# A long-lived pool on the other side of SBUF, residual pieces at later marks, and another opening order for attention, in a four-layer graph network kernel

## The chip, the core and the metric

The kernel is one launch on one core of one Trainium2 chip. The metric is the device time in microseconds (us), the median of the runs shown. A core has five engines that run their own instruction streams: TensorE (PE in the profile, with PEld for its weight loads), VectorE (DVE), ScalarE (ACT), GpSimd (POOL) and SyncE (SP). In this kernel SP does hardly anything but issue DMAs. On every engine the program's order is the order of execution, so an instruction that waits holds up all behind it on its engine.

## The reference, cut to what matters

x is 128 batches of 64 nodes with 256 channels in float32. Each of four layers adds its result to x. All of them begin with a norm over channels and a ReLU.

```python
h = relu(layernorm(x)); x = x + L0(h, adj)   # aggregate, W1, batch norm, ReLU, W2, batch norm
h = relu(layernorm(x)); x = x + L1(h, adj)   # two graph convolutions, then LSTMs
h = relu(layernorm(x)); x = x + L2(h)        # one head of causal attention over 64 nodes
h = relu(layernorm(x)); x = x + L3(h, adj)   # four heads of attention, masked by adj
# inside L1: for p = 1, 2, 3, 4 an LSTM over windows of p nodes replaces the last node of each window
```

## The kernel before, in words

The 8,192 rows are 16 chunks of 512 (`NCH`); two neighbours make a super-chunk (`SUP` = 2), so layer 1 has eight stages, sc = 0 to 7. The products of weight matrices are computed in Strassen's way with seven products, which is why so many small sums and copies on DVE, ACT and POOL stand between the matmuls.

**Pools.** SBUF has two stacks, left and right, and `pool(name, bufs, side)` opens a pool on top of one. A tile that comes to lie where older tiles lay waits for the last users of those. Layer 0 has `z1b` (64 KB per partition: 4 KB for each chunk), `w0` and, later, `stage` on the left, and `l0b` (24 KB) on the right: `w2_sb` (4 KB), `w2_sums` (4 KB) and two buffers of tag `h1` (8 KB each). Layer 1 then opens `lasting` (18 KB: `wg0_sb`, `wg1_sb` of 2 KB, `wih1_4` of 6 KB, two `cv` buffers of 4 KB), `w1` (46.5 KB: the third part of the single LSTM's weights and six buffers `wset` of 7 KB), `l1` (40 KB, its first tile `early`/`gates` of 16 KB) and, on the right, `l1r`. `lasting` lives until the end of the kernel.

**The opening of layer 1.** SP issues, in this order, `wg0_sb`, `wg1_sb` (in the profile `wg_sb`, L870 and L871), two bias loads (L874, L875), the two loads of x into `early` (L968), the single LSTM's weights (L888 to L890) and six `wset` loads (L905). `first_convolutions` makes chunks 0 and 1: tokens by transposes (L253), the sum with x (L979), a norm, and the aggregation (L228). Filler transposes (`keep_busy`) keep PE occupied in between.

**The stages of layer 1.** The LSTMs of a stage are a generator, `lstms(sc, hT)`. It stops at marks that are numbered through: 0 to 3 in the LSTM with p = 1 (`single`, matmuls at L1369), 4 to 7 in p = 2, 8 to 13 in p = 3, 14 to 21 in p = 4; half marks (4.5, 5.5, 8.5, 9.5, 11.5 ...) lie where a step's last product of its first two gates has been issued. At each mark the other work of the stage is taken one piece at a time from other generators, by tables of marks:

- `convolutions(c)`, 16 pieces: scale (L918); transposes (L1009), put to DRAM (L261), get (L268) and the load of x (L1016); `add_squares` (L298); two pieces of the norm's statistics (L195); two of its application on ACT (L210); aggregation (L228); copies (L1026); a product, its bound, a second product, its bias, an aggregation; and two pieces that write hT (L961). Tables `FIRST` (sc 0), `CONV`, and for the first pieces, taken a stage earlier, `BEGUN` and `BEGUN_FIRST` (sc 0).
- `residual(c)`, 3 pieces: four transposes of hT (L1309) and a put; a get; `add_squares` into x. Table `RESIDUAL`.
- `ahead(c)`, 7 pieces: a put and a get that put x in another order; two of statistics; two of application; transposes and a put. Tables `AHEAD`, `LATE`, `LATEST`, `FINAL`.

When several tables name one mark, the pieces run in this order: convolutions of the next stage, residual, ahead, begun convolutions.

**Weights.** Each p > 1 needs four `wset` tiles (gates in the order 0, 2, 3, 1), loaded by SP (L905) in a ring of six buffers: two in a p's last step just behind its half mark, two at its end. The two that are issued behind mark 11.5 are those of p = 4 for its third and fourth gates. p = 4 begins with a product for gates 0, 2 and 3 in turn (L1134, into y, y and x).

```python
each(A, pe(4), do("act", 2), do("act", 1))
yield "a"                        # a half mark: the pieces of that mark run here
each(B[:1], pe(3))
if last:
    load_sets(2)                 # two wset loads, L905, on SP
```

**The opening of attention.** Steps with names are written in an order by hand (`FIRST` in the last section, then `THIRD`, `ROUND` ...), `name+c` being step `name` for chunk c. `res1` and `pair1` are the pieces of the last two residuals and their reordering; `keep` puts x to DRAM; `norm3`, `apply3`, `chan3` are layer 3's norm, its application and PE transposes (L240); `q3x`, `k3x` its first products (L1528 on `w_sb`); `weights3` loads that weight (L1972); `load3` gets the transposed h of a later chunk. The step `table` is an Exp of one column (L1977).

Of the kernel before, what the change touches and what calls it, by code (L numbers as in the profile page):

```python
# [8 lines left out]
F32 = mybir.dt.float32  # L9
AF = mybir.ActivationFunctionType  # L10
# [3 lines left out]
P = 128  # L14
# [5 lines left out]
def kernel(  # L20
# [22 lines left out]
    nc = tc.nc  # L43
# [13 lines left out]
    SUP = 2  # L57
# [9 lines left out]
    small = ctx.enter_context(tc.tile_pool(name="small", bufs=4))  # L67

    def pool(name, bufs, side="left"):


        stack = ExitStack()
        return stack.enter_context(tc.tile_pool(name=name, bufs=bufs, side=side,
                                                reuse_waits="tile")), stack.close
# [72 lines left out]
    def keep_busy(n, name):  # L147

        ps = bank(f"idle_{name}")
        for i in range(n):  # L150
            nc.tensor.transpose(ps[:, :P], ident, ident)
# [106 lines left out]
    def put(mid, name, tag="far", bufs=12):  # L258

        far = dram.tile([P, Q, CH * KD // Q], F32, tag=tag, name=f"far_{name}", bufs=bufs)  # L260
        nc.sync.dma_start(far, mid)  # L261
        return far

    def get(dst, far):

        src = far.rearrange("(a t) b n -> b t a n", a=Q)
        for b in range(Q):
            nc.sync.dma_start(dst[b * 32 : (b + 1) * 32], src[b])  # L268
# [21 lines left out]
    def add_squares(dst, base, src):  # L290

        for h in range(2):
            q = slice(h * Q // 2, (h + 1) * Q // 2)

            def part(a):
                return a.rearrange("p j (k q c) -> p q (j k) c", k=KD, q=Q)[:, q]

            nc.vector.tensor_add(part(dst), part(base), src[:, q].rearrange("p q (n c) -> p q n c", c=32))  # L298
# [304 lines left out]
    with tc.manual_schedule(engines={mybir.EngineType.PE, mybir.EngineType.DVE,  # L603
# [69 lines left out]
        c = NCH - 1  # L673
# [175 lines left out]
    with tc.manual_schedule(engines={mybir.EngineType.PE}):  # L849
        c = NCH - 1  # L850
# [10 lines left out]


    xs = {}
    lasting, close_lasting = pool("lasting", 1)
    w1, close_w1 = pool("w1", 1)
    l1, close_l1 = pool("l1", 2)
    l1r, close_l1r = pool("l1r", 2, "right")
# [42 lines left out]
    hTs = {}  # L910
# [392 lines left out]
    def residual(c, hT):  # L1303

        i = c % SUP
        mid = l1r.tile([P, Q, CH * KD // Q], F32, tag="g", name=f"hm_{c}", bufs=3)
        for k in range(KD):
            for e in range(2):
                nc.vector.transpose(  # L1309
                    mid.rearrange("p (e h) (j k c) -> p k e j h c", e=2, j=NJ, k=KD)[:, k, e],  # L1310
                    hT[:, k, :].rearrange("p (h t i j e) -> p i e j h t", h=Q // 2, i=SUP, j=NJ,
                                          e=2)[:, i, e])
        far = put(mid, f"h{c}")
        yield
        dst = hT[:, i, :].rearrange("p (q n) -> p q n", q=Q)
        get(dst, far)
        yield
        add_squares(xs[c], xs[c], dst)
        yield
# [143 lines left out]
    def new_hT(sc):  # L1463

        hTs[sc] = l1r.tile([P, KD, SUP * CH], F32, tag="hT", name=f"hT_{sc}")
# [66 lines left out]
    def begin_attention():  # L1532

        tiles = [shared(f"{n}2_0") for n in ("hT", "q")]
        for w, i in ((wg0_sb, 0), (wg1_sb, 1)):
            nc.sync.dma_start(w, products_far[:, :, i * D : (i + 1) * D])
        load2(0, tiles[0].rearrange("p (q n) -> p q n", q=Q))
        st[0, "q2"] = tiles[1].rearrange("p (k n) -> p k n", k=KD)
        st[0, "v2"] = wih1[0].rearrange("p g s f -> p (g s f)")[:, : NJ * D].rearrange("p (j d) -> p j d", d=D)
        yield  # L1540
        for m in range(KD):
            nc.scalar.copy(st[0, "q2"][:, m, :], project_t(m, st[0, "hT2"], wg0_sb, "q2_0"))
            yield
        for t in range(NJ // 2):
            project_v(st[0, "v2"], st[0, "hT2"], wg1_sb, 0, "2_0", [t])
            yield
        new_hT(last + 1)
        load2(1, hTs[last + 1][:, 1, :].rearrange("p (q n) -> p q n", q=Q))
        st[1, "q2"] = hTs[last + 1][:, 0, :].rearrange("p (k n) -> p k n", k=KD)
        yield  # L1550
        for m in range(KD):
            nc.scalar.copy(st[1, "q2"][:, m, :], project_t(m, st[1, "hT2"], wg0_sb, "q2_1"))
            yield

    EARLY = 0, 3, 5, 7, 9, 9, 13, 15
    RESIDUAL = (0, 4, 5.5), (3, 5, 9)
    CONV = (3, 4, 5, 5.5, 7, 8, 9, 10, 10), (5, 5, 6, 9.5, 11, 11.5, 13, 14, 15, 15.5, 17, 18, 20)
    BEGUN = (11, 11, 14.5, 17, 17, 20, 21), (17.5, 19, 21)
    BEGUN_FIRST = (12, 14.5, 17, 19, 19, 20, 21), (20, 21, 21)
    FIRST = (1, 3, 3, 4, 4.5, 5, 5.5, 7, 8, 9, 9.5, 11, 11.5, 11.5), (2, 5, 8.5, 9, 9.5, 10, 11, 13, 14, 15, 15.5, 17, 17.5, 19, 20, 20)  # L1560
    AHEAD = (6, 7), (9, 10)
    LATE = (4.5, 4.5, 5.5, 9, 19.5), (9.5, 9.5, 11, 12, 21)
    LATEST = (4.5, 4.5, 5.5, 9, 9.5), (9.5, 9.5, 10, 11, 11.5)
    IDLE = {11: 8}
# [4 lines left out]
    with tc.manual_schedule(engines={mybir.EngineType.PE, mybir.EngineType.DVE, mybir.EngineType.Pool,  # L1569
# [3 lines left out]
        convs = {c: (convolutions if c >= SUP else first_convolutions)(c) for c in range(NCH)}  # L1573
# [17 lines left out]
    with tc.manual_schedule(engines={mybir.EngineType.PE, mybir.EngineType.DVE, mybir.EngineType.Pool,  # L1591
                                     mybir.EngineType.Activation, mybir.EngineType.SP}):
        last = NCH // SUP - 1
        lstm_tiles += [l1.tile(shape, F32, tag=tag, name=f"l_{tag}", bufs=1) for tag, shape in (
            ("gates", [P, 4, KD, CH]), ("cell", [P, KD, CH]), ("hs", [P, KD, CH]), ("hd", [P, 4, CH // 2]))]
        for sc in range(last + 1):
            todo = {}

            def units(places, unit):
                for n in places:  # L1600
                    todo.setdefault(n, []).append(unit)


            if sc < last:
                for i in range(SUP):
                    units((CONV if sc else FIRST)[i], convs[(sc + 1) * SUP + i])
                new_hT(sc + 1)
            if sc:
                for i in range(SUP):
                    units(RESIDUAL[i], residual((sc - 1) * SUP + i, hTs[sc - 1]))  # L1610
            else:
                units([0], convs[1])
            if sc > 1:
                for i in range(SUP):
                    units((LATEST if sc == last else LATE)[i], aheads[(sc - 2) * SUP + i])
            if sc:
                for i in range(SUP):
                    units((FINAL if sc == last else AHEAD)[i], aheads[(sc - 1) * SUP + i])
            if sc + 1 < last:
                for i in range(SUP):  # L1620
                    units((BEGUN if sc else BEGUN_FIRST)[i], convs[(sc + 2) * SUP + i])
            if sc == last:
                units(EARLY, begin_attention())
            n = -1
            for mark in lstms(sc, hTs[sc]):
                n = n + 0.5 if mark else int(n) + 1
                for u in todo.pop(n, ()):
                    next(u)
                if sc == last and n in IDLE:
                    keep_busy(IDLE[n], f"l{n}")  # L1630
            assert not todo
# [339 lines left out]
    def weights3(c):  # L1971
        nc.sync.dma_start(w3_sb, w3.rearrange("(k p) f -> p k f", p=P))  # L1972

    @step
    def table(c):

        nc.scalar.activation(small.tile([P, 1], F32, tag="table", name="table"),  # L1977
                             hTs[last][:, 0, :1], AF.Exp)


    ends = {NCH - SUP + i: residual(NCH - SUP + i, hTs[NCH // SUP - 1]) for i in range(SUP)}
    orders = {c: to_pairs(c) for c in ends}
    steps["res1"] = lambda c: next(ends[c])
# [52 lines left out]
    def store(c, t):  # L2036
# [3 lines left out]
        for r in range(2):  # L2040
# [16 lines left out]

    FIRST = """table+0 load2+2 score2+0 res1+14 v2a+1 v2b+1 res1+15 exp2+0 score2+1 divide2+0 q2+2 copyq2+2  # L2060
               exp2+1 turn2+0 divide2+1 load2+3 v2a+2 v2b+2 out2+0 keep+0 weights3+0 res1+14 res1+15 turn2+1
               norm3+0 score2+2 out2+1 keep+1 res1+14 res1+15 exp2+2 apply3+0 back+0 divide2+2 chan3+0
               pair1+14 pair1+14 turn2+2 q30+0 k30+0 norm3+1 pair1+15 pair1+15 out2+2 keep+2 q31+0 k31+0
               apply3+1 square3+1 score3+0 norm3+2 v3a+0 load3+1 v3b+0"""
    LAST = """exp3-2 sum3-2 load3+0 divide3-2 qa-1 q5-1 c11-1 v3a-1 qb-1 c12-1 qc-1 turn3-2 qd-1 out3-2
              score3-1 q30+0 store-2 back-1 k30+0 back+0 exp3-1 q31+0 sum3-1 k31+0 divide3-1 score3h+0
              v3b-1 exp3a+0 sum3a+0 turn3-1 exp3b+0 v3a+0 divide3a+0 out3-1 sum3b+0 divide3b+0 store-1
# [3 lines left out]
    def run(order, c):  # L2071
        for name in order.split():
            i = max(name.find("+"), name.find("-"))
            steps[name[:i]](c + int(name[i:]))

    with tc.manual_schedule(engines={mybir.EngineType.PE, mybir.EngineType.DVE,
                                     mybir.EngineType.Activation, mybir.EngineType.Pool,
                                     mybir.EngineType.SP}):
        run(FIRST, 0)
        close_l1r()  # L2080
        pool3, close_l3 = pool("l3", 2, "right")
# [8 lines left out]
        run(ROUND.replace("load2+1", "").replace("qd-2", "qd-2 sums_h-1"), NCH - 1)  # L2090
        run(LAST, NCH - 1)
    close_l2()
    close_lasting()
    close_l3()
    psum.pop()[2]()


# [44 lines left out]
```

## Time and profile before

| | us |
|---|---|
| median of 3 runs | 1902.86 (1902.72 to 1904.42) |
| profiled execution: its own time | 1900.71 |
| its span | 1898.9 |
| PE busy in the span | 1840.9 (97%) |
| DVE, ACT, POOL busy | 1319.9, 1053.2, 611.6 |
| mean granted PE clock | 0.991 |

A line of the timeline reads: start in us from the span's start, duration, engine and line, operation, output<-inputs, shapes, count; in brackets the idle time of that engine just before it, and what ended it. `SPq` is a DMA issue. A line of the waits view reads: engine, output and line that waited <- who ended it: us in total, times, the longest.

### The profile page before, as it was taken

What the parts mean: (1) busy time and instruction counts of PE and PEld (TensorE: products, weight loads), DVE (VectorE), ACT (ScalarE), POOL (GpSimd) and SP (SyncE); (2) the same over time, 40 slices, a digit from 0 to 9 for tenths busy, and PEclk for the clock granted to TensorE, in tenths of its full rate; (3) what the DMA queues carried; (4) which work ended last, traced back from release to release, by engine and by line L of the source; (5) the groups of instructions that cost most, each with busy time, mean ns of one, the idle gap of its engine ahead of it and who ended that gap; (6) DMA issues with size and microseconds to landing.
All of it is one profiled execution on the core that took longest, in us unless ns stands there. A gap on an engine that the chain in (4) does not pass through costs nothing.

```text
span 1898.9 us, 40682 instructions
## 1 busy us (share of the span) xinstructions
PE 1840.9 (97%) x15463; PEld 1513.1 (80%) x15463; DVE 1319.9 (70%) x3408; ACT 1053.2 (55%) x2502; POOL 611.6 (32%) x856
## 2 busy tenths in 40 slices
PE   8999988998999999999999999999999979999998
PEld 6877856985898799699699789789979847777776
DVE  6768845666667777767867866876667657777776
ACT  5766535555456565665655656656565634444453
POOL 5856623222212322422321422332132203332332
PEclk9999999998999999999999999999999989999999
DMA  3223642133433341432533433342244154444433
GB/s 114 79 69 142 213 182 73 59 110 123 133 134 123 106 161 52 148 127 89 178 123 112 165 118 130 145 131 104 84 133 141 38 162 146 134 151 141 143 112 112
DMA packets 113410, 234.48 MB, mean 123 GB/s; under 512 B 11712, under 2 KB 77120, under 8 KB 113216
## 3 DMA queue, kind: packets, MB, share of 16 engines
q1 hardware_dynamic: 112320, 230.02, 35.9%
q8 instruction: 123, 2.02, 0.4%
q0 software_dynamic: 320, 1.05, 0.2%
q10 hardware_dynamic: 576, 0.82, 0.1%
q14 instruction: 71, 0.58, 0.1%
HBM read 164.21 MB, written 67.63 MB: 122 GB/s over the span
## 4 chain that ended last, share of the span: by engine, by line
PE 83%; DVE 6%; ACT 5%; POOL 2%; issue 1%; DMA 1%; SPq 0%; DVEq 0%; ACTq 0%; POOLq 0%
PE x L1187 22%; PE z L1187 11%; PE v L1521 6%; PE y L1187 6%; PE y L1134 4%; PE v L936 3%; PE u L950 3%; PE p_q L1528 3%; PE X L1825 3%; PE X L437 2%; PE x L1134 2%; PE X L513 2%; PE x L1369 2%; PE y L1369 2%; PE Y L1825 1%
## 5 line engine op out<-in xcount | busy, mean ns | idle before, releaser
L1102 ACT ACTIVATE l_gates<-l_gates,bias 128x256 f32<-128x256 f32 (+4 forms) x528 | 238.1, 498 | 213.8 <-DVE l_gates L1196 111.8
L1187 PE MATMUL x<-xd,wset 128*128 128x128 f32 (+2 forms) x1152 | 255.4, 303 | 2.1 <-ACT l_gates L1193 1.7
L1187 PE MATMUL x<-l_hd,wset 128*128 128x128 f32 (+2 forms) x1152 | 254.6, 303 | 0.0
L1253 POOL TENSOR_TENSOR l_gates<-l_gates 128x512 f32<-128x512 f32 (+2 forms) x48 | 75.2, 1567 | 388.5 <-ACT l_gates L1102 388.5
L1187 PEld LDWEIGHTS x<-xd,wset 128*128 128x128 f32 x1152 | 187.7, 191 | 8.3 <-issue 1.4
L1187 PEld LDWEIGHTS x<-l_hd,wset 128*128 128x128 f32 x1152 | 187.8, 191 | 5.0
L1196 DVE TENSOR_TENSOR l_gates<-l_gates,x 128x128 f32<-128x128 f32 (+2 forms) x384 | 121.2, 321 | 99.8 <-PE x L1187 96.8
L1196 DVE TENSOR_TENSOR l_gates<-l_gates,z 128x128 f32<-128x128 f32 (+2 forms) x384 | 102.4, 318 | 124.3 <-PE z L1187 124.2
L1187 PE MATMUL z<-l_hs,wset 128*128 128x128 f32 (+2 forms) x768 | 147.0, 304 | 0.7 <-DVE l_hs L1111 0.7
L1187 PE MATMUL z<-hT,wset 128*128 128x128 f32 (+2 forms) x768 | 146.3, 303 | 0.0
L1193 ACT COPY l_gates<-y 128x128 f32<-128x128 f32 (+2 forms) x192 | 53.1, 290 | 142.5 <-PE y L1187 137.3
L1187 PEld LDWEIGHTS z<-l_hs,wset 128*128 128x128 f32 x768 | 116.8, 191 | 5.6 <-DVE l_hs L1111 2.3
L1187 PEld LDWEIGHTS z<-hT,wset 128*128 128x128 f32 x768 | 117.1, 191 | 3.3
L1102 ACT ACTIVATE l_gates<-x,bias 128x128 f32<-128x128 f32 (+2 forms) x216 | 84.7, 392 | 31.1 <-PE x L1187 28.4
L1187 PE MATMUL x<-hT,wset 128*128 128x128 f32 (+2 forms) x384 | 85.7, 305 | 0.0
L1187 PE MATMUL x<-l_hs,wset 128*128 128x128 f32 (+2 forms) x384 | 84.9, 303 | 0.0
L327 POOL TENSOR_TENSOR xd<-hT 128x128 f32<-128x128 f32 (+2 forms) x72 | 42.2, 587 | 129.1 <-DVE hT L1113 115.7
L1187 PE MATMUL y<-l_hd,wset 128*128 128x128 f32 (+2 forms) x384 | 83.6, 310 | 0.0
L1187 PE MATMUL y<-xd,wset 128*128 128x128 f32 (+2 forms) x384 | 82.6, 307 | 0.0
L1268 ACT ACTIVATE l_gates<-l_cell 128x256 f32<-128x256 f32 (+2 forms) x144 | 55.2, 383 | 42.5 <-DVE l_cell L1267 42.5
L1643 POOL TENSOR_TENSOR s<-s,mx 128x256 f32<-128x256 f32 (+2 forms) x33 | 40.4, 1225 | 118.9 <-DVE mx L1642 118.9
L1369 PE MATMUL x<-xd,wih 128*128 128x512 f32 x144 | 66.6, 609 | 8.9 <-DVE l_gates L1393 8.7
(358 smaller groups left out, 4557.5 us busy)
## 6 DMA issues: line engine op xcount, KB each, us to landing
wset<-wfar SPq DMA_DIRECT2D x96, 896.0 KB, 6.7
hT<-far_h SPq DMA_DIRECT2D x124, 128.0 KB, 3.2
far_h<-hm SPq DMA_DIRECT2D x16, 512.0 KB, 3.0
far_n<-xs SPq DMA_DIRECT2D x16, 512.0 KB, 4.0
xs<-far_n SPq DMA_DIRECT2D x64, 128.0 KB, 3.3
far_x<-xs SPq DMA_DIRECT2D x16, 512.0 KB, 3.0
x<-far_x SPq DMA_DIRECT2D x64, 128.0 KB, 3.3
xt<-in_x_dram SPq DMA_DIRECT2D x15, 512.0 KB, 3.9
```

The source lines that it names most:

```text
L936: nc.tensor.matmul(banks[m], wg0_sb[:, k, m * P : (m + 1) * P], agg[:, k, :], start=(k == 0), stop=(k == KD - 1))
L950: nc.tensor.matmul(banks[j // 2][:, j % 2, :], v[:, k, j * P : (j + 1) * P], wg1_sb[:, k, :], start=(k == 0), stop=(k == KD - 1))
L1102: nc.scalar.activation(gate(q, c, part), src, AF.Tanh if q == 2 else AF.Sigmoid, bias=bs[:, q * KD + c : q * KD + c + 1])
L1134: nc.tensor.matmul(folded(self.psum(kind)), wsets[p, self.q][:, BLOCKS[kind][0], :], ox[0][kind], start=kind in (1, 5), stop=True, skip_gr ...
L1187: nc.tensor.matmul(folded(self.psum(kind)), wsets[p, self.q][:, BLOCKS[kind][i], :], (ox[self.s] if part == "x" else oh)[kind], start=firs ...
L1196: nc.vector.tensor_add(gate(self.q, *dst), gate(self.q, *a), self.psum(kind))
L1253: nc.gpsimd.tensor_mul(gates[:, 0, :, :n], gates[:, 0, :, :n], gates[:, 2, :, :n])
L1268: nc.scalar.activation(gate(2, c, part), cells[:, c, part], AF.Tanh)
L1369: nc.tensor.matmul(folded(ps(g, kind)), single_block(KINDS1[kind])[:, g, :], right[kind], start=kind in (2, 5, 1), stop=True, skip_group_c ...
L1521: nc.tensor.matmul(ps[:, i, :], hT[:, k, j, :], w[:, k, first : first + D], start=(k == 0), stop=(k == KD - 1))
L1528: nc.tensor.matmul(ps.rearrange("p (a n) -> p a n", n=P), w[:, k, m * P : (m + 1) * P], hT[:, k], start=(k == 0), stop=(k == KD - 1))
L1825: nc.tensor.matmul(st[c, tag][:, i * CH // 2 : (i + 1) * CH // 2].rearrange("p (a n) -> p a n", n=P), w, st[c, "o7"][kind], start=first an ...
```

## The change

Four things change. `lasting` is opened on the right, below which `l1r` then lies; `w1` and `l1` start where `lasting` lay. Tables of marks change: the residual pieces move from (0, 4, 5.5), (3, 5, 9) to (0, 6, 9), (5.5, 7, 9.5) in stages 1 to 6 (stage 7 keeps the old ones under a new name); `AHEAD` moves accordingly; the second begun piece of the even chunk moves from mark 11 to 11.5; stage 0 uses `BEGUN` like all others, with its `FIRST` denser. Attention's opening order is rewritten, with `apply3+0`, `back+0` and `chan3+0` ahead of the gets and sums of `res1`, the Exp of chunk 0 earlier, and `weights3` behind `keep+1`. The step `table` goes.

```diff
-    lasting, close_lasting = pool("lasting", 1)
+    lasting, close_lasting = pool("lasting", 1, "right")
...
-    RESIDUAL = (0, 4, 5.5), (3, 5, 9)
+    RESIDUAL = (0, 6, 9), (5.5, 7, 9.5)
...
-    BEGUN = (11, 11, 14.5, 17, 17, 20, 21), (17.5, 19, 21)
-    BEGUN_FIRST = (12, 14.5, 17, 19, 19, 20, 21), (20, 21, 21)
-    FIRST = (1, 3, 3, 4, 4.5, 5, 5.5, 7, 8, 9, 9.5, 11, 11.5, 11.5), (2, 5, 8.5, 9, 9.5, 10, 11, 13, 14, 15, 15.5, 17, 17.5, 19, 20, 20)
-    AHEAD = (6, 7), (9, 10)
+    BEGUN = (11, 11.5, 14.5, 17, 17, 20, 21), (17.5, 19, 21)
+    RESIDUAL_LAST = (0, 4, 5.5), (3, 5, 9)
+    FIRST = (1, 1, 2, 2, 3, 4, 4, 5, 5.5, 7, 8, 9, 10, 10), (2, 3, 4.5, 5, 5, 6, 9.5, 11, 11.5, 13, 14, 15, 15.5, 17, 18, 20)
+    AHEAD = (9, 10), (10, 11)
...
-                    units(RESIDUAL[i], residual((sc - 1) * SUP + i, hTs[sc - 1]))
+                    units((RESIDUAL_LAST if sc == last else RESIDUAL)[i], residual((sc - 1) * SUP + i, hTs[sc - 1]))
...
-                    units((BEGUN if sc else BEGUN_FIRST)[i], convs[(sc + 2) * SUP + i])
+                    units(BEGUN[i], convs[(sc + 2) * SUP + i])
...
-    @step
-    def table(c):
-
-        nc.scalar.activation(small.tile([P, 1], F32, tag="table", name="table"),
-                             hTs[last][:, 0, :1], AF.Exp)
...
-    FIRST = """table+0 load2+2 score2+0 res1+14 v2a+1 v2b+1 res1+15 exp2+0 score2+1 divide2+0 q2+2 copyq2+2
-               exp2+1 turn2+0 divide2+1 load2+3 v2a+2 v2b+2 out2+0 keep+0 weights3+0 res1+14 res1+15 turn2+1
-               norm3+0 score2+2 out2+1 keep+1 res1+14 res1+15 exp2+2 apply3+0 back+0 divide2+2 chan3+0
-               pair1+14 pair1+14 turn2+2 q30+0 k30+0 norm3+1 pair1+15 pair1+15 out2+2 keep+2 q31+0 k31+0
-               apply3+1 square3+1 score3+0 norm3+2 v3a+0 load3+1 v3b+0"""
+    FIRST = """load2+2 score2+0 exp2+0 res1+14 v2a+1 v2b+1 score2+1 divide2+0 load2+3 q2+2 copyq2+2
+               turn2+0 exp2+1 v2a+2 out2+0 keep+0 divide2+1 norm3+0 v2b+2 turn2+1 score2+2 res1+15 out2+1
+               keep+1 exp2+2 weights3+0 divide2+2 apply3+0 back+0 chan3+0 res1+14 turn2+2 res1+15 norm3+1
+               q30+0 k30+0 out2+2 keep+2 res1+14 q31+0 res1+15 k31+0 apply3+1 pair1+14 pair1+14 square3+1
+               score3+0 norm3+2 pair1+15 pair1+15 v3a+0 load3+1 v3b+0"""
...
     close_l2()
+    close_l3()
     close_lasting()
-    close_l3()
```

The last lines close the two right-hand pools in the order of their stack.

## The prediction

> **What bounds the kernel now.** I read the page first, then PE's part of the waits view, then the granted clock, then the timeline around each wait, and SP's waits last.
>
> ```profile
> PE 1840.9 (97%) x15463; PEld 1513.1 (80%) x15463; DVE 1319.9 (70%) x3408; ACT 1053.2 (55%) x2502; POOL 611.6 (32%) x856
> PEclk9999999998999999999999999999999989999999
> ```
>
> PE is the bound: 1898.9 - 1840.9 = 58 us of idle time in the span, so the change, which touches no matmul, can win only idle time and slow clock. The clock has two visible dips (slices 10 and 33). In the clock record there are four stretches at 0.5: 253.4 to 260.2, 314.8 to 318.2, 451.3 to 461.6 and 1543.6 to 1557.2, each behind an idle PE. Where are the idle spells?
>
> ```profile
> PE tc_n L240 <- ACT h L187: 11.8, 1, 11.8
> PE x L1369 <- DVE l_gates L1393: 8.7, 1, 8.7
> PE y L1134 <- DVE l_gates L1141: 4.7, 8, 0.7
> PE agg_b L228 <- ACT cv L210: 4.5, 1, 4.5
> PE agg_b L228 <- ACT cv L187: 4.4, 1, 4.4
> ```
>
> Four waits of 29.4 us together are the ones ahead of those stretches: attention's opening, stage 0's end, and two aggregations in layer 1's opening and in stage 0. The third line is eight small ones at the start of p = 2. SP's waits show one line that belongs to the opening of layer 1:
>
> ```profile
> SPq L968 <- PE c L752: 12.3, 1, 12.3
> ```
>
> **What the Trainium skill says.** "TensorE: Matmul & The Clock Gate", section "What's actually happening", describes a clock that halves after an idle window of PE and is restored after a busy one. The trace agrees: the stretches last 6.8, 3.4, 10.2 and 13.7 us, behind waits of 4.4 to 11.8. The last and third are so long because the idle time lies partly in them. "DMA: Bandwidth & Descriptors", section "Two DMAs through the same engine are not ordered", has the issuing engine wait for the first DMA before a dependent one: here each put and get through DRAM holds SP for 2.8 us (put 848.05, get 850.85). "ScalarE: Activation LUTs", section "What ACT_TABLE_LOAD costs", prices a load at 1283 ns; the trace has 1.28. No page bears on a pool's reuse.
>
> **1. `lasting` on the right: +4.2 (2.6 to 5.8).** (+ is time won.) `early` lies 64.5 to 80.5 KB above the start of `z1b`, over `stage`, so SP holds L968 for L752 and issues at 244.54. Then the sum at L979 waits for the load, ending PE's 4.4 us. With `w1` (46.5 KB) at the start of `z1b`, `early` lies over chunks 11 to 15 of `z1b`, last read on ACT at 232.2. But `wg1_sb` now lies over the even `h1` buffer, which PE reads until 239.74 (L466); SP is held there, at L871. Its issue and those of the two biases and L968 (0.99 + 0.57 + 0.43) put the loads at about 241.8, 2.7 earlier, so L979 from 249.4 to 246.7 and PE's idle time from 4.4 to about 1.7. If that no longer drops the clock, 6.3 us of half-clock work save up to 3.1; I take 1.5. Low end: the idle time alone; 0 belongs to rival D.
>
> **2. Stage 0's denser first pieces: 0 (-2 to +2).** PE waits 4.4 at 314 and loses 1.7 more to the clock. With the apply piece at mark 2, close behind the norm, ACT waits about 1.1 for DVE's statistics and 1.9 for POOL's chain of four, with six ops of the single (3.15) behind it, on which PE waits. A new stall of that size takes the old one's place.
>
> **3. `BEGUN` in stage 0: +10.5 (9.5 to 11).** `BEGUN_FIRST` puts the odd chunk's get, x load and sum in one mark, 21:
>
> ```profile
> 451.29 0.43 SPq L1016 DMA_DIRECT2D xs<-in_x_dram  x1
> 455.78 1.29 DVE L298 TENSOR_TENSOR xs<-xs,cv 128x512 f32<-128x512 f32 x2 [9.87 <-DMA xs<-in_x_dram]
> 457.82 4.67 PE L1369 MATMUL x<-xd,wih 128*128 128x512 f32 x6 [8.65 <-DVE l_gates L1393]
> ```
>
> DVE waits 9.87 for the DMA, the single's sums (L1393) lie behind it, and PE stands 8.65. Its six matmuls take 4.67 against 2.74 in full clock. With get at 19 and sum at 21, as in stages 1 to 5, where this row has no wait, both go: 8.65 + 1.9.
>
> **4. Residual transposes of the odd chunk from 3 to 5.5: +3.8 (2 to 3.8).** At p = 2's start in stages 1 to 6 four transposes (2.11, L1309) stand ahead of the sums of L1141: 0.49 + 0.49 + 4 x 0.70 = 3.8.
>
> ```profile
> 778.96 2.11 DVE L1309 STREAM_TRANSPOSE hm<-hT 128x256 f32<-128x256 f32 x4
> ...
> 782.71 1.10 PE L1134 MATMUL y<-xd,wset 128*128 128x256 f32 x4 [0.70 <-DVE l_gates L1141]
> ```
>
> At 5.5 the sum that moves to 9 leaves DVE 3.3 idle, which covers 2.1; at 9.5 the 1.3 us sum meets 1.6 idle. If that cover fails, 6 x 0.5 goes back, which is the low end. On SP, the put, get and `AHEAD`'s put and get now stand ahead of p = 3's wset (issue 803.2, landed 807.9, needed 818.3); up to 2.8 later is harmless.
>
> **5. The begun transposes from 11 to 11.5: -14.9 (-3 to -22).** What is moved is two DVE transposes, a put, four gets and the x load, and behind them on SP stand the two wset loads of p = 4:
>
> ```profile
> 846.72 1.30 DVE L1009 STREAM_TRANSPOSE ym<-cv 128x512 f32<-128x512 f32 x2
> 848.05 0.34 SPq L261 DMA_DIRECT2D far_y<-ym  x1
> 850.85 1.73 SPq L268 DMA_DIRECT2D cv<-far_y  x4
> 850.91 1.28 DVE L1026 COPY cv<-agg_b 128x512 f32<-128x512 f32 x2
> 852.62 0.43 SPq L1016 DMA_DIRECT2D xs<-in_x_dram  x1
> 853.15 6.37 SPq L905 DMA_DIRECT2D wset<-wfar  x4
> ...
> 862.89 0.39 PE L1134 MATMUL x<-hT,wset 128*128 128x128 f32 x2
> ```
>
> At 11.5 the convolution's copies (850.91 to 852.2) come first, so the transposes move to 852.1, 5.4 later, and the weights with them. By the tile view of wset, issue plus landing against the first use is, in stages 1 to 5, 553.4/557.36, 707.3/709.86, 859.4/862.89, 1013.5/1016.42 and 1166.9/1169.69: slack 4.0, 2.6, 3.5, 2.9, 2.8, mean 3.16. PE then waits 5.4 - 3.16 = 2.2; taking the mean for stage 0 too, x 6 = 13.4. Each wait may cost half a clock window (up to 1.7); I take 1.5 in all. Low end: weights in time but for 0.5 a stage; high end: 2.2 and 1.5 each.
>
> **6. Attention's opening: +1.8 (0 to 5).** The chain now is one of sums and gets ahead of the norm:
>
> ```profile
> 1538.85 5.70 SPq L268 DMA_DIRECT2D hT<-far_h  x8
> 1546.75 1.29 DVE L298 TENSOR_TENSOR xs<-xs,hT 128x512 f32<-128x512 f32 x2 [4.77 <-DMA hT<-far_h]
> 1548.82 1.29 DVE L298 TENSOR_TENSOR xs<-xs,hT 128x512 f32<-128x512 f32 x2 [0.78 <-DMA hT<-far_h]
> 1550.04 0.16 DVE L185 SCALAR_TENSOR_TENSOR nmr_n<-mv_n,rstd_n 128x4 f32<-128x4 f32 x1
> 1550.88 2.80 PE L240 MATMUL tc_n<-ident,h 128*128 128x128 f32 x8 [11.84 <-ACT h L187]
> ```
>
> After: the norm's last step stands behind transposes (2.1), `out2+1`'s sums (1.3) and a divide (1.05) only, tc_n at about 1544.7. Then w_sb is late: behind `keep+1` it goes out at about 1543.3 (before 1538.4), lands 5.9 later, so p_q (L1528) starts at 1549.2 against 1553.9: +4.7. But `square3+1`'s put and `pair1+15` then stand on SP ahead of `load3+1`, which lands at about 1575, when PE, now early, wants it at about 1572: 2.9 goes back. Sum +1.8.
>
> **7. The step `table`: +0.2.** ACT loads a table twice for nothing (1.28 + 0.20 + 1.28 at 1381), beside matmuls; the only PE gap there is 0.3. If the load falls due in the opening instead, it is the 1.28 that Exp pays there anyway.
>
> **The sum.** 4.2 + 0 + 10.5 + 3.8 - 14.9 + 1.8 + 0.2 = +5.6. The profiled execution (1900.71, its span 1898.9) becomes 1895.1; it stands 2.15 below the median of 1902.86, which becomes 1897.3.
>
> **The rivals.**
> - **A, as summed (0.50).** Range 1892 to 1902, from the bounds of parts 1, 2 and 6 and a spread of 0.5 us a stage in part 5.
> - **B, the weights land in time (0.17).** Fewer DMAs beside the two loads, or transposes that run in a DVE gap ahead of the copies, bring the stall to 0.5 a stage. Part 5 is -3: 1897.3 - 11.9, some 1885. For it: landings vary, 5.7 to 7.2. Against: all five slacks lie below 5.4.
> - **C, slower: late weights each time with a dropped clock (0.18).** Place: the product into x of p = 4, six times. The rest wins 20.5, so it decides from 20.5 / 6 = 3.4 us a stage. A stall of 2.6 with 1.7 of slow clock gives 4.3, or 25.8 in all: 1902.86 - 20.5 + 25.8, about 1908. For it: 2.1 us of idle time was enough ahead of 451.3.
> - **D, the change doesn't do what it says in the openings (0.15).** SP stays held in layer 1's opening by the user that lies under another tile of the moved pools, and attention's late w_sb eats its gain: parts 1 and 6 are 0, 1902.86 + 0.4, about 1903; with part 2 at its low end 1905.
>
> **How the numbers follow.** About 0.2% (3.8 us) is what a measurement of this kernel can tell from no change. A lies above 1899.06 in some 3 of 10 cases: faster 0.35, same 0.15. B is faster 0.17; C slower 0.18; D same 0.10, slower 0.05. Together faster 0.52, same 0.25, slower 0.23. The range takes in B's and C's points, 1884 to 1909; the likeliest case has 1892 to 1902 alone.
>
> **What would show it.** Part 1: L968 issued near 242 and no PE wait of 4.4 behind L979. Part 3: no L1369 wait of 8.7. Part 4: L1141 gone from the waits of p = 2. Part 5: a new wait of PE at L1134 for wset, six times, about 2 us each, wset issued some 5 us later than before; its absence is B, a row of 0.5 clock behind each is C. Part 6: w_sb's landing as the wait of p_q. The forecast is wrong if PE's idle sum falls by over 15 us, or if stage 0 shows new waits of over 5 us together behind ACT's norm.

## The result and the profile after

The change makes no measurable difference: the ratio of after to before is 0.9998, with a 95% interval of 0.9981 to 1.0015. The medians are 1902.34 us after and 1902.79 us before (four runs each). The profiled execution of after took 1903.54, its span 1901.8; it is one of the longer runs of after (1900.77 to 1903.54), as that of before (1900.71) is one of the shorter.

The time is the same, and yet PE's part of the waits view is another one. Every wait of over 3 us in the view of before is gone or cut, and new ones stand there:

```profile
PE x L1134 <- DMA wset<-wfar: 14.9, 6, 3.4
PE x L1134 <- ACT l_gates L1374: 5.4, 1, 5.4
PE tc_n L240 <- ACT h L187: 5.1, 1, 5.1
PE Z L1825 <- DMA hT<-far_h: 3.0, 1, 3.0
...
PE p_q L1528 <- DVE st_n L159: 1.4, 1, 1.4
...
PE agg_b L228 <- ACT cv L187: 1.3, 2, 1.1
```

The first line is the six waits for late weights; the second is new in stage 0; the next three (tc_n, Z, p_q) belong to attention's opening; the last is what is left of 4.4 in layer 1's opening. `Z` is the first product that reads the h which `load3+1` fetches. The waits of 8.7 (L1369) and of L1141's 0.7 have shrunk to a few tenths. The second line's cause stands on ACT, whose apply piece waits for POOL's end of the norm, with the single's last six operations behind it:

```profile
297.64 1.09 ACT L210 ACTIVATE cv<-xs,nmr_b,rstd_b 128x256 f32<-128x256 f32 x2 [3.62 <-POOL nmr_b L203]
```

On the page PE is busy for longer, and the dip of the clock in the tenth slice is gone, for all that the clock record has seven stretches at 0.5 in place of five (one at the very end in both):

```profile
PE 1845.0 (97%) x15463; PEld 1519.0 (80%) x15463; DVE 1323.1 (70%) x3408; ACT 1052.1 (55%) x2499; POOL 613.0 (32%) x856
...
PEclk9999999999999999999999999999999989999999
```

They lie at 298.9 (6.8 us), 391.0, 548.0, 858.6, 1015.7 (3.4 each), 1541.3 (13.7) and 1899.7. Four follow waits for weights; the tenths of a slice (47 us) are too coarse to show 3.4.

Where was time won and lost? The view by stretches of time answers, cut where PE is at about the same work; only at 295 is after already 3.3 us further on, so the first two rows are to be read together. First before, then after. The columns are the stretch, its length, and the busy time of PE, PEld, DVE, ACT and POOL with their instructions, then the clock, the share of DMA, and GB/s. The rows are layer 1's opening, stage 0, stages 1 to 7, and attention.

```profile
230.00:295.00 65.00, 57.72 (x444) 36.28 (x443) 33.82 (x78) 28.56 (x55) 15.55 (x21) 0.95 0.46 164
295.00:461.90 166.90, 151.12 (x1132) 129.97 (x1131) 101.66 (x290) 85.64 (x228) 39.34 (x59) 0.96 0.27 96
461.90:1531.00 1069.10, 1060.75 (x7810) 909.54 (x7808) 762.64 (x2138) 631.32 (x1650) 297.96 (x433) 1.00 0.35 120
1531.00:1898.90 367.90, 347.80 (x4201) 261.08 (x4200) 251.32 (x531) 157.46 (x289) 104.69 (x128) 0.98 0.46 140
```

```profile
230.30:295.00 64.70, 59.48 (x453) 35.98 (x451) 37.38 (x87) 30.36 (x57) 15.57 (x21) 1.00 0.47 165
295.00:449.20 154.20, 146.47 (x1121) 129.51 (x1121) 98.42 (x279) 82.96 (x222) 40.22 (x59) 0.97 0.28 102
449.20:1531.00 1081.80, 1064.98 (x7812) 915.38 (x7811) 763.98 (x2137) 631.16 (x1650) 298.90 (x434) 1.00 0.35 119
1531.00:1901.80 370.80, 350.17 (x4201) 261.37 (x4199) 252.79 (x533) 157.36 (x289) 104.02 (x127) 0.98 0.47 139
```

Opening and stage 0 together are 13.0 shorter (231.9 against 218.9). Stages 1 to 7 are 12.7 longer: PE's idle time there goes from 8.4 to 16.8, and its busy time grows by 4.2, while three stretches of slow clock lie there that before does not have. Attention is 2.9 longer. What stage 0 wins, the next five stages give back.

How they give it back stands in stage 3 of the timeline:

```profile
843.36 1.28 DVE L1026 COPY cv<-agg_b 128x512 f32<-128x512 f32 x2
844.56 1.29 DVE L1009 STREAM_TRANSPOSE ym<-cv 128x512 f32<-128x512 f32 x2
845.88 0.34 SPq L261 DMA_DIRECT2D far_y<-ym  x1
848.68 3.26 SPq L268 DMA_DIRECT2D cv<-far_y  x4
851.98 0.43 SPq L1016 DMA_DIRECT2D xs<-in_x_dram  x1
852.51 2.54 SPq L905 DMA_DIRECT2D wset<-wfar  x4
...
858.92 0.77 PE L1134 MATMUL x<-hT,wset 128*128 128x128 f32 x2 [3.41 <-DMA wset<-wfar]
```

The copies now come first on DVE, the transposes behind them, then put, get and load of x, and only then the weights. They go out at the same time by the clock as before (about 853), but PE is 7.5 us further on in its work, stands 3.41 for them, and its clock then halves at 858.6.

In layer 1's opening, SP's wait for L752 at L968 (12.3) is down to 0.2, and another line of SP's waits has taken its place:

```profile
SPq L871 <- PE z L466: 8.1, 1, 8.1
```

The row is that of the `h1` buffer under `wg1_sb`. SP issues L968 at 240.63, 3.9 earlier.

### The profile page after: what moved, and what is told of

It is laid out like the page before. It is cut to its first block, busy times and chain, and to the rows that moved or that the text cites. A ratio compares the mean times of both kernels' runs of the same rounds, so it can differ in the third digit from the quotient of the medians.

```text
span 1901.8 us, 40668 instructions
## 1 busy us (share of the span) xinstructions
PE 1845.0 (97%) x15463; PEld 1519.0 (80%) x15463; DVE 1323.1 (70%) x3408; ACT 1052.1 (55%) x2499; POOL 613.0 (32%) x856
## 4 chain that ended last, share of the span: by engine, by line
PE 85%; DVE 6%; DMA 3%; ACT 2%; POOL 2%; issue 1%; SPq 0%; DVEq 0%; ACTq 0%; POOLq 0%
PE x L1187 21%; PE z L1187 11%; PE y L1187 6%; PE v L1521 5%; PE y L1134 4%; PE x L1369 4%; PE y L1369 3%; PE u L950 3%; PE x L1134 3%; PE p_q L1528 3%; PE X L1825 3%; PE X L437 2%; DMA wset<-wfar 2%; PE X L513 2%; PE v L936 2%; PE z L1134 2%
## 5 line engine op out<-in xcount | busy, mean ns | idle before, releaser
L327 POOL TENSOR_TENSOR xd<-hT 128x128 f32<-128x128 f32 (+2 forms) x72 | 42.7, 594 | 126.6 <-DVE hT L1113 114.3
L1141 DVE TENSOR_TENSOR l_gates<-l_gates,y 128x256 f32<-128x256 f32 (+2 forms) x144 | 46.4, 343 | 46.5 <-PE y L1134 42.9
```

## The experiments

The first four ask what the six waits hang on, and what stage 0 is worth. The edits are against after (`u_`) or before (`o_`); a `v_` run adds its edit to the run that its line names. In the expectations T is the explanation put forward, R a rival to it. Gains worked out in us are the ratio times the median of before in the same runs.

**u_begun**, the one mark undone:

```diff
-    BEGUN = (11, 11.5, 14.5, 17, 17, 20, 21), (17.5, 19, 21)
+    BEGUN = (11, 11, 14.5, 17, 17, 20, 21), (17.5, 19, 21)
```

> The kernel after with the second begun piece back at mark 11 (all else as after). Theory T (the pieces at 11.5 stand ahead of the two wset loads of p = 4 on SP, and PE waits for these): the six waits of 14.9 us and the four stretches of slow clock behind them (4 x 1.7 = 6.8) go, 1902.3 - 21.7 = 1880.6, between 1878 and 1885; no PE wait on wset. Rival R1 (it is the residual and reordering pieces, moved to marks 9 to 11, that hold SP or load the DMA engines): waits on wset stay at 1 us or more a stage and the time stays above 1892.

Measured: 1881.78, ratio to before 0.9889 (0.9874 to 0.9903), so 21.1 faster than before and some 20.6 faster than after. No wait of PE for wset is left; the largest are those of stage 0 and attention, in the waits view:

```profile
PE x L1134 <- ACT l_gates L1374: 5.4, 1, 5.4
PE tc_n L240 <- ACT h L187: 5.1, 1, 5.1
PE Z L1825 <- DMA hT<-far_h: 3.2, 1, 3.2
```

One entry in a table of marks costs all that the rest of the change wins. R1 falls: the residual and reordering pieces are where the change put them, and SP reaches the weights in time.

**u_weights_first**, the pieces stay at 11.5, but the two loads go ahead of them on SP:

```diff
+            if last and p == 3:
+                load_sets(2)
             yield "a"
             each(B[:1], pe(3))
-            if last:
+            if last and p != 3:
                 load_sets(2)
```

> The kernel after with the pieces still at 11.5, but for p = 3 the two wset loads are issued on SP ahead of that mark's pieces. T says only the order on SP counts: the wset loads go out some 5 us earlier against their use, no wait of PE on wset, 1879 to 1886, as with mark 11. Rival R2 (the put, gets and load of x beside the weights slow their landing, wherever they stand in the queue): waits of 1 to 2 us a stage stay, above 1890.

Measured: 1881.91, ratio 0.9888 (0.9872 to 0.9905), the same as with mark 11, and no wait for wset. Its SP in stage 1:

```profile
529.66 0.91 SPq L905 DMA_DIRECT2D wset<-wfar  x2
531.30 0.32 SPq L261 DMA_DIRECT2D far_y<-ym  x1
538.48 1.74 SPq L268 DMA_DIRECT2D cv<-far_y  x4
```

So the wait is one of order in SP's queue, not of DVE's transposes, nor of the mark as such. R2 falls for the loads. What takes longer is the put, off the path: behind two weight loads it needs 7.1 us to land (531.30 to 538.42) in place of 2.8, and PE does not wait for it.

**o_begun**, the same mark moved in the kernel before, alone:

```diff
-    BEGUN = (11, 11, 14.5, 17, 17, 20, 21), (17.5, 19, 21)
+    BEGUN = (11, 11.5, 14.5, 17, 17, 20, 21), (17.5, 19, 21)
```

> The kernel before with one edit alone, the second begun piece from 11 to 11.5 (stages 1 to 5; stage 0 has its own table). T: five waits on wset of 1.7 to 3.4 us, 13 in all, and some three or four stretches of slow clock of 1.7 each: 1902.8 + 18 = 1921, between 1915 and 1924. R1: without the moved residual pieces SP reaches the weights in time, below 1908.

Measured: 1920.18, ratio 1.0089 (1.0074 to 1.0104): 16.9 slower, with five waits (the row of its waits view below) and three stretches of slow clock behind them (561.5, 718.6, 875.6; 3.4 each):

```profile
PE x L1134 <- DMA wset<-wfar: 12.1, 5, 3.3
```

12.1 + 3 x 1.7 = 17.2. The price comes alone, without the rest of the change.

**o_stage0**, the tables of stage 0 alone:

```diff
-                    units((BEGUN if sc else BEGUN_FIRST)[i], convs[(sc + 2) * SUP + i])
+                    units(BEGUN[i], convs[(sc + 2) * SUP + i])
```

with the new `FIRST`, and 11, 11 in `BEGUN`. The two tables were not tried apart: the begun pieces at 11 ask for the `cv` buffers that the old `FIRST` still holds at 11.5.

> The kernel before with the new tables of stage 0 alone: the denser FIRST, and BEGUN (still with 11, 11) in place of BEGUN_FIRST. T: the wait of 8.65 at L1369 and its slow clock (10.2 us long, about 2 us lost beyond the wait) go; the wait of 4.5 at the aggregation with its 3.4 us of slow clock is replaced by one of 5.4 at x of p = 2 with 6.8 us of slow clock, 2.6 lost; the small waits 0.85 and 0.42 go. Net 10.6 + 1.3 - 2.6 = 9.3 won: 1893.5, between 1890 and 1896. Rival R3 (denser pieces hold up DVE and ACT elsewhere in stage 0 and take it back): above 1899.

Measured: 1887.99, ratio 0.9919 (0.9904 to 0.9934), 15.4 faster, against an expected 9.3. R3 falls. In the profiled executions the span is 12.3 shorter, and stage 0 by itself 12.5 (166.9 to 154.4): PE's idle time falls by 10.3 and its busy time by some 2. The wait at L1369 is gone, the one of 5.4 is there. The two small waits expected to go, 0.85 and 0.42, went. Slow clock accounts for about 1 of the 2: 7.1 us of busy time lay at half clock in stage 0 before (3.4 behind 314.8, 3.7 from 457.8), 5.1 here (304.7 to 309.8), and each costs half of itself. The rest is open.

The next four take the other parts alone, and repair one.

**o_right**, `lasting` on the right in the kernel before:

```diff
-    lasting, close_lasting = pool("lasting", 1)
+    lasting, close_lasting = pool("lasting", 1, "right")
```

> The kernel before with lasting on the right alone (and the pools closed in that order). T: SP's wait at L968 (12.3) goes and one of 8 at L871 takes its place, L968 goes out near 241, PE's wait of 4.4 at agg_b falls to about 1.1 and the slow clock ahead of the stages goes: 3.3 + 1 won, which a PE in program order keeps to the end: 1903.1 - 4.2 = 1898.9, between 1896 and 1901. Rival R4 (what is won waits again at the aggregation of stage 0, L210 at 314, or at a transfer): within 1 us of before.

Measured: 1900.25, ratio 0.9988 (0.9980 to 0.9996), 2.3 faster. Both theories hold a part. PE is 3.7 ahead at 264 and still 2.9 at 446, but at the end of stage 0 it stands for the same late transfer, and for longer than before:

```profile
451.11 0.75 SPq L1016 DMA_DIRECT2D xs<-in_x_dram  x1
455.71 1.29 DVE L298 TENSOR_TENSOR xs<-xs,cv 128x512 f32<-128x512 f32 x2 [12.71 <-DMA xs<-in_x_dram]
457.75 2.90 PE L1369 MATMUL x<-xd,wih 128*128 128x512 f32 x3 [11.50 <-DVE l_gates L1393]
```

The matmul starts at 457.75, against 457.82 in before: in that profile, the slowest of o_right's 13 runs (1897.4 to 1903.7), the lead is gone whole. SP issued the put ahead of this load 2.9 earlier (443.02 against 445.94), yet its get followed only at 449.13, 6.1 us later in place of 3.3; why the put took longer was not tried. In after, where this wait no longer exists, the lead lasts.

**o_resid**, the residual tables and `AHEAD` alone (stage 7 keeps the old residual table, as in the change):

```diff
-    RESIDUAL = (0, 4, 5.5), (3, 5, 9)
+    RESIDUAL = (0, 6, 9), (5.5, 7, 9.5)
...
-    AHEAD = (6, 7), (9, 10)
+    AHEAD = (9, 10), (10, 11)
```

> The kernel before with the residual tables and AHEAD alone. T: the six waits of 0.5 to 0.7 at the start of p = 2 (L1141) go and nothing takes their place: 1903.1 - 3.8 = 1899.3, between 1897 and 1901. Rival R5 (the sum at 9.5 and the put and gets at 9 to 11 hold up DVE or the loads of the weights): new waits at L1134 of as much, 1902 to 1906.

Measured: 1897.03, ratio 0.9971 (0.9960 to 0.9982), 5.5 faster. PE's lead over before grows from stage to stage, from 0 at 477 over 0.7, 1.4, 2.3 and 3.3 to 4.2 at 1243. L1141's waits are down to one of 0.4, and R5's new ones do not come.

**o_att**, attention's new order and no step `table`, alone (the diff is that of the change).

> The kernel before with attention's new opening and without the step table, alone. T: tc_n starts some 6.6 us earlier (wait 5.1 in place of 11.8), p_q waits for w_sb or the statistics by 1.4 to 2.4, Z waits 3 for the gets that stand on SP behind pair1+15; from Z on PE is where it was: within 1.5 us of before, 1901.6 to 1904.6. Rival R6 (the waits at Z come from the late stages' DMAs in the kernel after, not from this order): no wait at Z, 1897 to 1899.

Measured: 1906.20, ratio 1.0015 (1.0007 to 1.0022), 2.9 slower, where PE was expected to be level from Z on. R6 falls. The three waits are there as expected: 5.1 at tc_n, 2.1 at p_q, and 4.1 at Z. What was not expected is slow clock behind Z (3.4 us at 1580.1), and more lost behind it.

**v_first**, u_begun with one apply piece of stage 0 a mark later:

```diff
-    FIRST = (1, 1, 2, 2, 3, 4, 4, 5, 5.5, 7, ...
+    FIRST = (1, 1, 2, 3, 3, 4, 4, 5, 5.5, 7, ...
```

> The kernel after with the begun piece at 11 and, in stage 0, the even chunk's first apply piece at mark 3 in place of 2, behind the single's last six operations on ACT. T (ACT stands waiting for POOL's chain of the norm with these six behind it, and PE's x bank behind them): the wait of 5.4 at x of p = 2 and its 6.8 us of slow clock go, less up to 1 at the aggregation: 1881.8 - 8 = 1873.8, between 1872 and 1877. Rival R7 (the aggregation at mark 4 then waits for the apply pieces instead): a wait at agg_b of 3 to 5, above 1878.

Measured: 1880.62, ratio 0.9881 (0.9866 to 0.9896), which is not to be told from u_begun (0.9889). The place is right: ACT is free again, and x of p = 2 waits 0.72 in place of 5.43. But the next product then waits for POOL:

```profile
296.05 2.38 POOL L100 TENSOR_TENSOR rstd_b<-rstd_b,mhalf 128x4 f32<-128x4 f32 x1
298.51 0.20 POOL L202 TENSOR_TENSOR nmr_b<-mv_b,rstd_b 128x4 f32<-128x4 f32 x1
298.80 0.24 POOL L203 TENSOR_SCALAR nmr_b<-nmr_b 128x4 f32<-128x4 f32 x1
299.00 0.73 POOL L327 TENSOR_TENSOR xd<-hT 128x256 f32<-128x256 f32 x1
...
299.79 1.50 PE L1134 MATMUL z<-xd,wset 128*128 128x256 f32 x4 [3.13 <-POOL xd L327]
```

This is the timeline of v_first. The norm's chain stands on POOL ahead of the operands of p = 2. It was hidden behind the wait on ACT. (Of the 3.13, 1.2 is L100 itself, which took 1.17 in u_begun.) R7's place was wrong, its kind right. Against u_begun PE is 3.6 ahead at 1524 in v_first, of which 1.5 are left at 1591: Z waits 4.0 instead of 3.2.

The last four take attention's opening apart, and put the repairs together.

**o_att_load3**, o_att with one step moved ahead of two:

```diff
-               score3+0 norm3+2 pair1+15 pair1+15 v3a+0 load3+1 v3b+0"""
+               score3+0 norm3+2 load3+1 v3a+0 pair1+15 pair1+15 v3b+0"""
```

> The kernel before with attention's new opening (and no step table), as in the third run of the last four, but with load3+1 ahead of both pieces of pair1+15 on SP. T6 (the put and the gets of pair1+15 hold SP till 1574.4 while the h that load3+1 fetches has lain in DRAM since 1570.9): load3's gets go out 3.5 us earlier, Z's wait of 4.1 and the slow clock behind it go; against 1906.2 that is 4 to 6 less, 1900 to 1902.5. Rival R8 (the two puts issued within 0.4 us of each other share the DMA engines, each lands after 5 to 6 us, and the gets are as late as ever): Z still waits 2 or more, 1904 to 1907.

Measured: 1900.87, ratio 0.9993 (0.9984 to 1.0001), against 1.0015 without the move: 4.2 less. Z waits no more. SP first in o_att, then here:

```profile
1565.81 0.34 SPq L261 DMA_DIRECT2D far_h<-mid  x1
1566.19 0.43 SPq L261 DMA_DIRECT2D far_n<-xs  x1
1572.54 1.79 SPq L279 DMA_DIRECT2D xs<-far_n  x4
1574.44 1.79 SPq L268 DMA_DIRECT2D hT<-far_h  x4
```

```profile
1564.53 0.34 SPq L261 DMA_DIRECT2D far_h<-mid  x1
1569.01 1.89 SPq L268 DMA_DIRECT2D hT<-far_h  x4
1570.94 0.43 SPq L261 DMA_DIRECT2D far_n<-xs  x1
```

From the put of far_h to its gets it was 8.6 us and is 4.5. Another round trip through DRAM stood between a put and its own get: in o_att far_h had landed at 1570.9, 3.5 ahead of its gets. R8's times do not come; its mechanism, two puts that slow each other, is not tested by this, since the move also parts the puts, from 0.4 us to 6.4.

**u_att**, u_begun with attention's old order, less `table` (the diff is that of the change, the other way).

> The kernel after with the begun piece at 11 and the old order of attention's opening (without the step table). T6 (the new order costs some 3 us by Z's late gets and their slow clock): below 1881.8 by 2 to 4, 1878 to 1880; wait of 11.8 at tc_n back, none at Z. Rival R6 (the cost of the new order in the kernel before comes from old residual tables): at 1883 or above, since the wait at tc_n is back.

Measured: 1878.58, ratio 0.9873 (0.9860 to 0.9886), against 0.9889: 3.0 less by the ratios, whose intervals overlap. It agrees with o_att from the other side; R6 was to be at 1883.

**v_all**, v_first with the opening repaired in three places:

```diff
-  ... out2+0 keep+0 divide2+1 ... score2+2 res1+15 out2+1 keep+1 exp2+2 weights3+0 divide2+2 apply3+0 back+0 ...
+  ... out2+0 keep+0 weights3+0 divide2+1 ... score2+2 res1+15 apply3+0 out2+1 keep+1 exp2+2 divide2+2 back+0 ...
-               score3+0 norm3+2 pair1+15 pair1+15 v3a+0 load3+1 v3b+0"""
+               score3+0 norm3+2 load3+1 v3a+0 pair1+15 pair1+15 v3b+0"""
```

> The kernel after with the begun piece at 11, the first apply piece at mark 3 in stage 0, and in attention's opening weights3 behind keep+0, apply3+0 ahead of out2+1, and load3+1 ahead of pair1+15. T: against 1880.6 without the three last edits, Z's wait of 4.0 goes, tc_n waits about 2.8 in place of 5.1, p_q no more, and one stretch of slow clock (1.7) goes: 8 less at most, 1873 to 1877. Rival R9 (attention's rounds are bound by a chain behind PE, so that an earlier start is given back as waits later): 1879 to 1881.

Measured: 1872.11, ratio 0.9841 (0.9827 to 0.9854), 30 us faster than before and after alike, and 7.6 faster than v_first. Z's and p_q's waits are gone, tc_n's longest is 2.9, and the stretch of slow clock there is 6.8 us in place of 10.2 and 3.4. R9 falls.

**v_pool**, v_all with the norm's chain behind the operands on POOL:

```diff
-    FIRST = (1, 1, 2, 3, 3, 4, 4, 5, 5.5, 7, ...
+    FIRST = (1, 1, 3, 4, 4, 4.5, 5, 5, 5.5, 7, ...
```

> The last version (1872.1) with stage 0's even chunk once more later: the second statistics piece at mark 3 and the apply pieces at 4, the aggregation at 4.5. T7 (in that version POOL's norm chain, 3.3 us, stands ahead of the sums of p = 2's operands at L327, for which PE waits 3.1): the sums go first, the wait of 3.1 and its 3.4 us of slow clock (1.7) go: 1867.5, between 1866 and 1870. Rival R10 (the aggregation, now half a mark later, waits for the apply pieces on ACT instead): a wait of 2 to 4 at agg_b, 1871 to 1874.

Measured: 1878.51, ratio 0.9867 (0.9850 to 0.9883), so 5 slower than v_all by the ratios. The wait at L327 went, and agg_b waits only 0.97. But the copies of that aggregation now queue on DVE behind the LSTM's steps, with the product for the same mark right behind them on PE:

```profile
315.47 1.28 DVE L1026 COPY cv<-agg_b 128x512 f32<-128x512 f32 x2
...
316.80 3.78 PE L936 MATMUL v<-cv,wg_sb 128*128 128x512 f32 x4 [7.06 <-DVE cv L1026]
```

7.1 and a stretch of 10.2 us at half clock took the place of 3.1 and 3.4. Neither T7 nor R10 named this place. v_all is the best version that was run.

## Why the prediction was right where it was, and where not

The forecast was 1897.3, with 1884 to 1909 around it, and faster at 0.52. The measured 1902.34 lies in the range, but outside the likeliest case's 1892 to 1902; the outcome was "same", to which 0.25 was given. By its parts (us won; those measured are of the parts run alone on before, with their intervals):

| part | forecast | measured alone |
|---|---|---|
| 1 pool | +4.2 | +2.3 (0.8 to 3.8) |
| 2 and 3 stage 0 | +10.5 | +15.4 (12.6 to 18.3) |
| 4 residual | +3.8 | +5.5 (3.4 to 7.6) |
| 5 begun, stages 1 to 5 | -12.4 (five sixths of 14.9) | -16.9 (14.1 to 19.8) |
| 6 and 7 attention | +2.0 | -2.9 (-4.2 to -1.3) |

These add to +3.4; with stage 0's own wait for weights, which o_begun leaves out and the trace of after has (2.27 and a stretch of 1.7), to -0.6. The whole change has +0.4, so the parts account for it, as closely as intervals of this width can tell. That the total came within 5 us of the forecast is in part luck: stage 0 and the residuals brought 6.6 more than forecast, the pool, the begun pieces and attention 11.3 less, and stage 0's own wait 1.5 less (forecast 2.5).

- **Part 1** held in its place: `wg1_sb` over `h1`, SP held at L871, L968 at 240.6 (forecast 241.8; in after the two biases went out ahead of L871, at 229.7 and 230.4), agg_b down to 1.1. In after PE is 3.9 ahead behind it. Alone on before it pays less, since the later wait at L1369 absorbs it.
- **Part 2** forecast a new stall of the same size in the old one's place, on ACT behind POOL's chain. It is 5.4 against 4.5, with 6.8 us of slow clock against 3.4. ACT waits 3.62 there, forecast 1.1 + 1.9. The prediction had named new waits of over 5 us in stage 0 behind ACT's norm as a sign that it is wrong. They came, and did not decide the total, since part 3's gain beside them was larger. **Part 3** held: the wait of 8.7 is 0.4. Together they brought some 5 more than the sum by the medians, 2 by the traces.
- **Part 4** held: six waits of 3.8 gone, cover intact.
- **Part 5** is the step that failed, by a size. Its mechanism, place and count were right: six waits at x, 14.9 in all, forecast 13.4. The term that was mis-sized is the slow clock behind them. I put it at 1.5 for all six; four of six were followed by a stretch of 3.4 at half clock, up to 1.7 each, 6.8 in all. u_begun, where both go, is 20.6 faster than after, 21.7 by this count, not 14.9. The single shift of 5.4 held in the mean only: the time from the first of the two loads issued to its first use, less the stall, shrank in stages 1 to 5 by 5.2, 5.2, 6.7, 5.8 and 3.9, which is 5.4 in the mean.
- **Part 6** failed in its sign. tc_n came at 1544.3 (forecast 1544.7) and p_q at 1549.0 (1549.2), but of that lead 0.35 was left at Z, not 1.8. The wait of p_q, forecast for w_sb, is put down to DVE's st_n in after (1.4); w_sb landed within 0.2 us of its end, and is the one named in u_begun and o_att (2.3 and 2.1). The profile of before showed the transfers on SP that would stand ahead of `load3+1`, and I priced them as a delay of a lead. o_att shows that they cost more than the lead, with slow clock behind Z, and o_att_load3 that the order on SP is the cause of Z's wait. Behind Z some 2 to 3.5 us more are lost (2.5 in after against before), which no run here settles. L1904 has waits there that the profile gives no cause for: 0.6 to 2.4 in the six profiles with the old opening (before 0.6), 2.4 to 3.6 in the eight with the new.
- **Part 7** has no run of its own; its +0.2 is neither shown nor refuted.

Of the rivals, C described the mechanism best: stalls with slow clock behind them. It decided from 3.4 us a stage, and (14.9 + 6.8) / 6 is 3.6 by the trace, 20.6 / 6 = 3.4 by the times. The case lay on the break-even point itself. B is refuted by the six waits. D is refuted for layer 1's opening; for attention's it has the direction right, where the gets' place on SP ate the gain (o_att_load3). How much of it w_sb's place took was not tried alone.

## What to carry to other kernels

When a piece with a put and a get is moved, list what is issued behind it on the DMA-issuing queue: here the piece itself had time to spare, and two weight loads queued behind it did not; issuing them first costs nothing. A stall of over 2 us on a saturated matmul engine is to be priced with the slow clock that may follow it, here up to 1.7 more in four cases of six, and whether it follows hangs on how the stall falls on the clock's windows (next section). A change that mixes gains and losses in separate stages is worth taking apart even when its sum is nil: undoing one mark won 21 us, and repairing the next waits in turn some 9 more.

## What the runs showed that was not expected

A wait of PE of 2.19 us (stage 1) was followed by 3.4 us of half clock, one of 2.50 (stage 2) and one of 1.66 (stage 5) by none. The Trainium skill ("TensorE: Matmul & The Clock Gate", "What's actually happening") puts the slow state behind an idle window of about 3.4 us, and has the windows run on without regard to a kernel's start. The second half the clock records bear out: in each of the fourteen profiles all switches of the clock lie on one grid of 3.413 us, within 4 ns, and the grid's place against the start differs from profile to profile (0.8 us in before, 1.9 in after). The first half does not hold as it stands: a window idle for 2.2 was enough. PE's busy time, and after it the granted clock and DMA, in four of after's windows:

```profile
544.61:548.03 3.42, 1.23 (x11) 1.00 1.02 420
698.21:701.63 3.42, 2.31 (x9) 1.00 1.06 407
701.63:705.04 3.41, 2.02 (x18) 1.00 1.01 423
1169.25:1172.67 3.42, 1.76 (x16) 1.00 1.02 420
```

Stage 1's stall leaves 2.19 idle in one window, and the next one is slow. Stage 2's longer stall is cut by a boundary at 701.63 into windows with 1.11 and 1.39 idle, and stage 5's leaves 1.66: no slow clock. Over all fourteen profiles, away from the ends of the run, each of the 49 full-clock windows with 1.96 or more idle was followed by a slow one; of the 94 with 0.9 to 1.77, three were. So the same stall can cost 1.7 more or nothing, as it happens to fall.

Two smaller things:

- A put that was issued behind two weight loads took 7.1 us to land instead of 2.8; the put of `pair1+15`, 0.4 us behind another, took 6.0 (1566.19 to 1572.17 in o_att).
- The same small power on POOL (L100, 128x4) took 1.04 us in before and 2.38 in v_first and v_all. Its cause was not tried.
